# Eight groups of edges, counted back from the end from the fifth group on instead of the sixth

## The chip, the cores and the metric

The program runs on one core of a Trainium2 chip. The time is device microseconds of that core for one execution, from the runs listed below. Engines are called as in the profile: PE (matmul; its weight loads are PEld), DVE (vector), ACT (scalar), POOL (GpSimd) and SP, whose queue here only issues DMAs.

## The reference

206,250 edges, each with a row of 128 float32 and a node number `src` from 0 to 6249 in no useful order; 6,250 nodes with a row `x` of 128 float32. Everything is float32.

```
edge_aggr = zeros((n, 128)).at[src].add(edge_features)        # scatter-add of edge rows to nodes
combined  = concat([x, edge_aggr, global]) @ W_c + b_c
h = softplus(combined @ W1 + b1)
h = softplus(h @ W2 + b2)
out = layernorm(x + h @ W3 + b3)
```

## The kernel before

The scatter-add is done as a sort and a sum, the three layers follow.

**Buckets.** The nodes are cut into 32 buckets of 196. A DRAM table `rows_by` has a room of fixed size for each bucket, and sorted edge rows (128 values and the node's place in its bucket, padded to 136 floats, 544 bytes) are written into it. A *chunk* is 128 rows of one bucket, 68 KB.

**Columns, pairs, groups.** The edges lie as 1,692 columns of up to 128 edges; two columns are a pair. The 846 pairs form 8 groups, `GROUPS = (28, 72, 124, 124, 124, 128, 124, 122)`. So the groups begin at columns 0, 56, 200, 448, 696, 944, 1200 and 1448.

**Positions.** For each group, DVE and PE find where each edge goes. `node_codes(g)` splits node numbers into bucket and place. `positions(g)` records steps: compare 16 columns with the buckets (`count_set`, L498), count them with small matmuls (L509), make starts (L527 to L551), running totals for all sets (L586 to L611), then ranks inside a set (L557, L559, L576) and the target of each pair of rows (L727, L742). For a group below `GAP` these are one list of steps, and rows are placed from the front of each room. For a group from `GAP` on (`split`) there are two lists: part 0 counts, and part 1, which can begin when all groups to the end have been counted, ranks and places; the totals run over the split groups alone, and the rows are placed so that they end at the end of each room. Part 1 compares the 16 columns again. `ahead_of[g]` says which lists are worked off while group g is scattered, spread over the first 0.85 of its time by `over`.

**Sort.** Per pair, PE multiplies rows of edges by a one-hot matrix (L1155), ACT copies the result to one of six sets (L1167), and POOL scatters it to `rows_by` with an indirect DMA (L1184), 846 in all. The rows come by SP, 16 columns in a load of 1032 KB (`rows<-in_edge`).

**Fills.** Since a bucket's number of rows is random, between what is placed from the front and what is placed to the end there is a stretch of which it isn't known beforehand whether rows come. `fill_rows` writes -1 there ahead of the scatters (`rows_by<-fill`, 23 DMAs on SP). Each has a due pair, which is never later than the first pair of group `GAP`, and they are spread in time from 30 us up to 60 us ahead of the last due pair.

**Sums.** `sum_steps` plans loads of up to 8 chunks (`chunks<-rows_by` on SP, six buffers), a one-hot of the place in the bucket for up to 4 chunks (DVE, L990), a matmul for each chunk (PE, L1013) and an addition to `sums_t` (DVE, L1036). Which chunks may be loaded after how many columns is bounded from below by chance: up to `gap_at` (the first column of group `GAP`) counted from the front, after it from the end:

```
rows = (per * col - below(group_of(col))[k] if col <= gap_at
        else room * P - per * (NC - col) - left(group_of(col))[k])
```

A load waits on the SP queue for the scatters up to its column. The 196 chunks whose column is 1692 wait for all of them.

**Order.** Every step has a planned time (a scatter 1.3 us after the one before, a chunk 0.58 us of PE); the steps are sorted by it, and this order is the program of PE, DVE, ACT and SP. Sum steps that are planned after the last scatter are left for `node_layers`, which mixes them with the layers (L1358 and L1359 first layer, L1362 second, L1397 third).

Of the kernel before, what the change touches and what calls it, by code (L numbers as in the profile page):

```python
# [7 lines left out]
F32 = mybir.dt.float32  # L8
# [10 lines left out]
P = 128  # L19
# [11 lines left out]
ROWS_SD, MIXED_SD = 2.016, 0.5  # L31
LEAST, LEAST_MIXED = 3.9, 3.6
ABOVE, ABOVE_MIXED, ABOVE_LEFT = 500.0, 100.0, 1200.0
GAP = 5
TARGETS = (1, 3, 5, 8, 10, 13, 15, 18, 20, 23, 25, 28, 30, 33, 36, 38)

LOAD_COLS = 16
# [109 lines left out]
def kernel(  # L147
# [43 lines left out]
    G = len(groups)  # L191
    B_MAX = max(GROUPS)
# [12 lines left out]
    def left(g):  # L205
        n = NC - 2 * groups[g][0]
        return LEAST * ROWS_SD * n ** 0.5, LEAST_MIXED * MIXED_SD * n ** 0.5
# [3 lines left out]

    gap_at = 2 * groups[GAP][0]

# [20 lines left out]
    def untouched(k, per):  # L234
        return max(0, int(per * (NC - gap_at) - left(GAP)[k] - 2))

# [82 lines left out]
    with ExitStack() as phase:  # L319
# [3 lines left out]
        per = phase.enter_context(tc.tile_pool(name="per", bufs=2))  # L323
# [22 lines left out]
        enough = keep.tile([KB, Q_MAX], F32, name="enough")  # L346
        beyond = keep.tile([KB, G - GAP + 1, 4], F32, name="beyond")
        shift = keep.tile([KB, 2], F32, name="shift")
        whole_of = keep.tile([KB, 2, 2], F32, name="whole_of")

        def scratch(name):
            return per.tile([P, 4 * P], F32, name=name, bufs=1)

        def whole_nodes(part, n):
            node = scratch("first")[:part.shape[0], :n]
            wrap = scratch("second")[:part.shape[0], :n]
            nc.vector.tensor_copy(node, part)
            nc.vector.tensor_scalar(wrap, node, 0.0, float(N), op0=ALU.is_lt, op1=ALU.mult)
            nc.vector.tensor_add(node, node, wrap)
            nc.vector.tensor_scalar(node, node, -1.0, float(N), op0=ALU.max, op1=ALU.min)  # L360
            nc.vector.tensor_scalar(wrap, node, 0.0, float(N + 1), op0=ALU.is_lt, op1=ALU.mult)
            nc.vector.tensor_add(part, node, wrap)
            return part, node, wrap
# [7 lines left out]
        def node_codes(g):  # L371

            s0, s1 = groups[g]
            if s1 > s0:
                a, b = 2 * s0, 2 * s1
                part, node, wrap = whole_nodes(pair_i[:, a:b], b - a)
                quot_i = wrap.bitcast(I32)
                nc.vector.tensor_scalar(quot_i, part, 1.0 / BL, 0.5 / BL - 0.5, op0=ALU.mult,
                                        op1=ALU.add)
                over = scratch("third")[:PN, :b - a]  # L380
                nc.vector.scalar_tensor_tensor(node, quot_i, -float(BL), part,
                                               op0=ALU.mult, op1=ALU.add)
                nc.vector.tensor_scalar(over, node, BL - 0.5, None, op0=ALU.is_gt)
                nc.vector.scalar_tensor_tensor(over, node, -0.5, over,
                                               op0=ALU.is_lt, op1=ALU.subtract)
                nc.vector.scalar_tensor_tensor(pair_low[:, a:b], over, float(BL), node,
                                               op0=ALU.mult, op1=ALU.add)
                if b > NF:
                    c = max(a, NF)
                    nc.vector.tensor_scalar(quot_i[:, c - a:], quot_i[:, c - a:], dump[:PN], None,  # L390
                                            op0=ALU.max)
                m = a + (b - a) // BLOCK * BLOCK
                nc.vector.tensor_tensor(by_quad(pair_block[:, a:m]), by_pair(quot_i[:, :m - a]),
                                        by_pair(over[:, :m - a]), op=ALU.subtract)
                if m < b:
                    nc.vector.tensor_sub(pair_block[:, m:b], quot_i[:, m - a:], over[:, m - a:])
# [54 lines left out]
        def positions(g):  # L451
# [5 lines left out]

            split = g >= GAP

# [14 lines left out]
            def opened():  # L474
                if sets:
# [4 lines left out]
                    own["alone"] = per.tile([KB, Q_MAX], BF16, name="alone", bufs=1)  # L480
                    late, deep = ("_late", G - GAP) if split else ("", 1)
                    own["starts"] = per.tile([KB, 2, Q_MAX], F32, name="starts" + late, bufs=max(2, deep))
# [106 lines left out]
            def all_sets2():  # L589
# [4 lines left out]
                for k in range(2):  # L594
                    nc.vector.tensor_tensor_scan(total[:, k, :quads], enough[:, :quads],
                                                 small[:, 2 * k], totalled[k], op0=ALU.min, op1=ALU.add)
                    totalled[k] = total[:, k, quads - 1:quads]
                    if g in (GAP - 1, G - 1):
                        nc.vector.tensor_copy(whole_of[:, split, k:k + 1], totalled[k])
# [466 lines left out]
        def node_rows():  # L1066

            banks_of, v = {}, nc.vector

            def product_of(name, *pairs):  # L1070
                small = banks_of[name] = small_bank()
                for k, (of, by, w) in enumerate(pairs):
                    nc.tensor.matmul(small[:, k, :w], of, by, start=True, stop=True)

            def got(name, k=0, w=1):
                return banks_of[name][:, k, :w]

            b2_all = []

            def b2_rows():  # L1080
                b2_all.append(per.tile([P, P], F32, name="b2_all", bufs=1))
                v.tensor_scalar(b2_all[0], ones, b2_c, None, op0=ALU.mult)

            return [
                lambda: product_of("c", (of_weights["wc2"], cols[:, 3:4], 1)),
                lambda: product_of("fold", *((of_weights[f"wc{k}"], w_sb["w1"], D) for k in range(2))),
                lambda: v.tensor_add(c_bias, got("c"), cols[:, 0:1]),
                lambda: v.tensor_copy(fold, banks_of["fold"][:, :2, :]),
                lambda: product_of("z", (w_sb["w1"], c_bias, 1)),
                lambda: None,  # L1090
                lambda: v.tensor_add(z_bias, got("z"), cols[:, 1:2]),
                lambda: v.tensor_scalar(neg_z, z_bias, -1.0, None, op0=ALU.mult),
                lambda: product_of("b2", (w_sb["w2"], z_bias, 1)),
                lambda: None,
                lambda: v.tensor_add(b2_c, got("b2"), cols[:, 2:3]),
                lambda: v.tensor_scalar(neg_b2, b2_c, -1.0, None, op0=ALU.mult),
                b2_rows,
                lambda: product_of("b3", (b2_all[0], w_sb["w3"], D)),
                lambda: None,
                lambda: v.tensor_add(b3_all, got("b3", w=D), of_weights["b3"]),  # L1100
            ]
# [94 lines left out]
        with tc.manual_schedule(engines={ET.PE, ET.DVE, ET.Activation, ET.SP}):  # L1196
            by_part = src.rearrange("(p t) -> p t", p=P)

            def src_cols(a, b):
# [7 lines left out]
                name=nc.get_next_instruction_name(), act_func_set_id=TABLES))  # L1207
# [91 lines left out]
            when(begins[last_pair], count_over)  # L1299
            when(ends[-1], lambda: fills_left())  # L1300
            nodes, held = node_rows(), 0
            ahead_of = {g: [(g + 1, 0)] for g in range(G - 1)}
            ahead_of[GAP - 1] = [(GAP, 1)]
            for k in range(GAP, G):
                ahead_of[k - 3].insert(-1 if k == G - 1 else 1, (k, 0))
            for k in range(GAP + 1, G):
                ahead_of[k - 1] = [(k, 1)]
            ahead_of[G - 1], position_steps = [], {}
            for g in range(G):
                mine = [q for q in range(len(pieces)) if pieces[q][0] == g]  # L1310
                t0 = begins[mine[0]]
# [307 lines left out]
```

## Time and profile before

| | us |
|---|---|
| runs (3) | 1279.74, 1282.51, 1284.93; median 1282.51 |
| the profiled execution | 1280.91 |
| its span, first to last instruction | 1279.1 |
| PE busy | 1156.0 (90%) |
| DVE busy | 1047.0 (82%) |
| ACT busy | 913.4 (71%) |
| POOL busy | 883.6 (69%) |
| DMA | 381.95 MB, mean 299 GB/s |

A row of the timeline has the start, the time, engine, line and operation, what is written and read, and in brackets the idle time of the engine before it and what ended it. A row of a table by stage has the stretch, its length, busy time and count of each engine asked for, the granted share of the PE clock, the mean busy share of the 16 DMA engines, and GB/s. PE's records of a float32 matmul come in twos: 3,516 records of L1013 are 1,758 chunks.

### The profile page before, as it was taken

The numbers are of one execution on the slowest core, as the hardware profiler recorded it, in microseconds if no ns is written. First come the engines' busy times: TensorE is split into PE (matmuls) and PEld (weight loads), VectorE is DVE, ScalarE is ACT, GpSimd is POOL, SyncE is SP. The second block draws the span as 40 slices with busy tenths as digits, with TensorE's granted clock in tenths as the row PEclk, the third lists the DMA queues.
The fourth block names the chain that finished last, engine by engine and source line by source line (L and its number), as shares of the span: only waits on it lengthen the run. The fifth ranks groups of instructions, "written<-read, shape, count | busy, mean of one in ns | idle before, by whom it ended". The sixth has DMA issues, their size and how long they took to land.

```text
span 1279.1 us, 26170 instructions
## 1 busy us (share of the span) xinstructions
PE 1156.0 (90%) x8617; PEld 1098.4 (86%) x8617; DVE 1047.0 (82%) x2289; ACT 913.4 (71%) x2150; POOL 883.6 (69%) x915
## 2 busy tenths in 40 slices
PE   5777898797998899989899999999999999899893
PEld 4677788787998898989899999999999999898772
DVE  7878979986789898899888887789877767687784
ACT  5887877886776688866987878877888888303343
POOL 2777777776777777777777777777777777750334
PEclk9988999998899899999999999999999999999996
DMA  6789999999999989997999999999999999875421
GB/s 242 249 304 357 334 314 306 346 340 334 338 347 331 333 315 336 322 315 266 320 317 312 313 340 329 337 319 332 322 350 335 363 343 355 286 234 144 142 69 54
DMA packets 174635, 381.95 MB, mean 299 GB/s; under 512 B 27546, under 2 KB 118626, under 8 KB 160670
## 3 DMA queue, kind: packets, MB, share of 16 engines
q1 hardware_dynamic: 130751, 260.70, 61.7%
q0 software_dynamic: 41328, 115.65, 23.3%
q10 hardware_dynamic: 2415, 3.85, 0.8%
q8 instruction: 72, 1.18, 0.4%
q14 instruction: 69, 0.57, 0.1%
HBM read 242.47 MB, written 142.20 MB: 301 GB/s over the span
## 4 chain that ended last, share of the span: by engine, by line
PE 62%; DVE 11%; DMA 11%; ACT 6%; issue 5%; POOL 4%; SPq 0%; ACTq 0%; DVEq 0%; POOLq 0%
PE part L1013 37%; PE sorted L1155 20%; DMA rows_by<-pairs,pair 7%; POOL rows_by L1184 4%; ACT pairs L1167 3%; DMA chunks<-rows_by 3%; DVE hot L990 2%; ACT sort_hot L1142 1%; PE small L557 1%; PE small L559 1%; DVE past L727 1%; DVE sort_hot L1139 1%; PE small L1397 1%; PE sorted L1362 1%; DVE slot L576 1%
## 5 line engine op out<-in xcount | busy, mean ns | idle before, releaser
L1184 POOL DMA_INDIRECT rows_by<-pairs,pair x846 | 830.5, 982 | 289.3 <-issue 208.1
L1167 ACT COPY pairs<-sorted 64x387 f32<-64x387 f32 (+2 forms) x1144 | 543.5, 475 | 224.0 <-PE sorted L1155 165.1
L1013 PE MATMUL part<-hot,chunks 128*128 128x196 f32 x3516 | 671.0, 334 | 16.0 <-DVE sums_t L1036 9.0
L1013 PEld LDWEIGHTS part<-hot,chunks 128*128 128x128 f32 x3516 | 577.4, 191 | 25.2 <-DVE sums_t L1036 10.7
L1155 PE MATMUL sorted<-rows,sort_hot 122*128 122x129 f32 x3384 | 489.6, 284 | 36.3 <-ACT pairs L1167 25.3
L1155 PEld LDWEIGHTS sorted<-rows,sort_hot 122*128 122x128 f32 x3384 | 448.9, 196 | 45.7 <-ACT pairs L1167 35.7
L990 DVE TENSOR_TENSOR hot<-chunks,both_ps 128x784 f32<-128x784 f32 (+3 forms) x541 | 427.1, 810 | 11.7 <-DMA chunks<-rows_by 7.7
L1036 DVE TENSOR_TENSOR sums_t<-sums_t,part 128x392 f32<-128x392 f32 (+1 forms) x262 | 143.6, 548 | 115.9 <-PE part L1013 113.0
L1142 ACT ACTIVATE sort_hot<-plain,slot 122x128 f32<-122x128 f32 x684 | 227.9, 392 | 8.8 <-DVE slot L576 5.9
L1139 DVE TENSOR_TENSOR sort_hot<-slot,both_ps 122x768 f32<-122x768 f32 (+2 forms) x172 | 159.6, 928 | 7.7 <-PE sorted L1155 7.4
L1144 ACT ACTIVATE sort_hot<-sort_hot 122x768 f32<-122x768 f32 x114 | 95.9, 841 | 0.2
L1439 POOL TENSOR_SCALAR y<-y,mv,rs 128x128 f32<-128x128 f32 x40 | 31.3, 788 | 91.1 <-DVE rs L1427 90.8
L576 DVE TENSOR_REDUCE slot<-small 122x16 f32<-122x512 f32 (+2 forms) x109 | 72.9, 669 | 16.5 <-PE small L559 16.0
L498 DVE TENSOR_TENSOR pair_ib<-pair_block,plain 122x512 bf16<-122x512 bf16 (+2 forms) x157 | 63.5, 411 | 0.2
L1369 ACT ACTIVATE away<-sorted,z_bias 128x512 f32<-128x512 f32 (+2 forms) x13 | 8.5, 656 | 71.8 <-DMA chunks<-rows_by 46.4
L557 PE MATMUL small<-pair_ib,half 122*122 122x512 bf16 (+2 forms) x109 | 42.6, 391 | 9.9 <-DVE slot L576 9.6
L742 PEld LDWEIGHTS <-past 128*128 128x128 f16 x424 | 24.7, 98 | 22.6 <-DVE past L727 17.8
L742 PE MATMUL small<-jump,past 128*128 128x56 f16 (+3 forms) x424 | 28.8, 188 | 16.3 <-DVE past L727 12.1
L727 DVE TENSOR_TENSOR past<-both_ps,starts 128x512 f16<-128x512 f32 (+1 forms) x61 | 39.7, 666 | 0.2
L559 PEld LDWEIGHTS <-starts_h 128*122 128x122 bf16 x236 | 24.9, 146 | 13.2 <-issue 8.7
L727 DVE TENSOR_TENSOR past<-both_ps,starts_late 128x512 f16<-128x512 f32 (+2 forms) x49 | 32.4, 662 | 0.0
L1116 ACT COPY rows<-pair_i 122x16 f32<-122x16 f32 x106 | 22.3, 211 | 7.8 <-DMA rows<-in_edge 6.9
(161 smaller groups left out, 516.7 us busy)
## 6 DMA issues: line engine op xcount, KB each, us to landing
rows<-in_edge SPq DMA_DIRECT2D x105, 1032.0 KB
chunks<-rows_by SPq DMA_DIRECT2D x362, 136.0 KB
chunks<-rows_by SPq DMA_DIRECT2D x203, 204.0 KB
chunks<-rows_by SPq DMA_DIRECT2D x75, 272.0 KB
rows_by<-pairs,pair POOLq DMA_INDIRECT x846
rows_by<-fill SPq DMA_DIRECT2D x10, 1249.5 KB
rows_by<-fill SPq DMA_DIRECT2D x10, 714.0 KB
chunks<-rows_by SPq DMA_DIRECT2D x13, 408.0 KB
```

The costliest lines, as they stand in the source:

```text
L498: nc.vector.tensor_tensor(ib, cols.unsqueeze(2).to_broadcast([PN, m, SB, QUAD]), bucket_at[:PN].unsqueeze(1).to_broadcast([PN, m, SB, QUAD ...
L576: nc.vector.tensor_reduce(to, of, axis=mybir.AxisListType.X, op=ALU.max)
L727: nc.vector.tensor_tensor(past[:, :, a:b], twice_ps[:KB].unsqueeze(1).unsqueeze(1).to_broadcast([KB, 2, b - a, P // 2]), own["starts"][:, ...
L990: nc.vector.tensor_tensor(hot[:, q - a:q - a + m], chunks[j][:, lo:hi + 1:step, D:W].to_broadcast([P, m, BL]), iota_ps.unsqueeze(1).to_bro ...
L1013: nc.tensor.matmul(part[:, b - base_of[v], :], t[:, place_in(j, q), :D], hot[:, q - a], start=first, stop=last)
L1036: nc.vector.tensor_add(here, here, of)
L1139: return [lambda: nc.vector.tensor_tensor(hot[:PN, :2 * m], slot[:PN, at:at + 2 * m].unsqueeze(2).to_broadcast([PN, 2 * m, P]), slot_ps[:P ...
L1142: return [lambda j=j: nc.scalar.activation(hot[:PN, j], by_slot[:PN], AF.Abs, bias=slot[:PN, at + j:at + j + 1], scale=-1.0) for j in rang ...
L1144: for j in range(2 * m)] + [lambda: nc.scalar.activation(hot[:PN, :2 * m], hot[:PN, :2 * m], AF.Relu, bias=1.0, scale=-1.0)]
L1155: nc.tensor.matmul(out[:, j, :], hot[:PN, at], rows_at[col // LOAD_COLS][:PN, col % LOAD_COLS, :], start=True, stop=True)
L1167: nc.scalar.copy(sets_at[i][64 * n:64 * n + 64, lo:lo + m, h, :W], out[64 * h:64 * h + 64, :m, :])
L1184: s = nc.gpsimd.indirect_dma_start(out=dst, out_offset=bass.IndirectOffsetOnAxis(ap=at, axis=0), in_=rows[:, j].rearrange("p a b -> p (a b ...
```

## The change

`GAP` becomes 4: group 4 (columns 696 to 943) is split as groups 5 to 7 are, placed from the end and counted in advance. Which group's time counts which is now a table:

| steps | before, in the time of group | now |
|---|---|---|
| group 3, all | 2 | 2 |
| group 4, all | 3 | - |
| group 4, part 0 | - | 2 |
| group 4, part 1 | - | 3 |
| group 5, part 0 | 2 | 2 |
| group 6, part 0 | 3 | 3 |
| group 7, part 0 | 4 | 3 |
| groups 5, 6, 7, part 1 | 4, 5, 6 | 4, 5, 6 |

The scratch tiles of `node_codes` have 256 columns instead of 512 (a group has at most 256). Tiles of the split groups exist four times instead of three.

```
-GAP = 5
+GAP, COUNTED_IN = 4, {4: 2, 5: 2, 6: 3, 7: 3}
...
-            return per.tile([P, 4 * P], F32, name=name, bufs=1)
+            return per.tile([P, 2 * B_MAX], F32, name=name, bufs=1)
...
-            ahead_of = {g: [(g + 1, 0)] for g in range(G - 1)}
-            ahead_of[GAP - 1] = [(GAP, 1)]
+            ahead_of, position_steps = {g: [(g + 1, 0)] if g + 1 < GAP else [] for g in range(G)}, {}
+            for k, g in COUNTED_IN.items():
+                ahead_of[g].append((k, 0))
             for k in range(GAP, G):
-                ahead_of[k - 3].insert(-1 if k == G - 1 else 1, (k, 0))
-            for k in range(GAP + 1, G):
-                ahead_of[k - 1] = [(k, 1)]
-            ahead_of[G - 1], position_steps = [], {}
+                ahead_of[k - 1].append((k, 1))
```

`gap_at` follows from `GAP`: column 696 instead of 944. The fills' due pairs and the columns after which chunks may be loaded follow from that.

## The prediction

> **What bounds the kernel now.** I read the page's slices first, then the groups, then busy time by stage, then the end of the timeline. Slices first (tenths of 40 slices of 32 us):
> ```profile
> PE   5777898797998899989899999999999999899893
> POOL 2777777776777777777777777777777777750334
> L1184 POOL DMA_INDIRECT rows_by<-pairs,pair x846 | 830.5, 982 | 289.3 <-issue 208.1
> ```
> POOL is flat at 7 until 1120 us: one scatter after another, 0.98 us each and then mostly a pause that waits for nothing ("issue"). Two neighbours give the pitch, and the last of the 846 shows the end of this stage:
> ```profile
> 1119.21 0.98 POOL L1184 DMA_INDIRECT rows_by<-pairs,pair  x1 [0.30 <-issue]
> 1120.49 0.97 POOL L1184 DMA_INDIRECT rows_by<-pairs,pair  x1 [0.30 <-issue]
> ```
> So a scatter takes 1.28 us at best, and 846 of them 1083 us. Where is more spent? The scatters alone, by stage (columns: stretch and its us, POOL busy and count, clock, DMA share, GB/s):
> ```profile
> 152.00:282.00 130.00, 98.67 (x101) 0.96 0.93 326
> 282.00:473.00 191.00, 138.16 (x141) 0.95 0.95 334
> 473.00:640.00 167.00, 127.17 (x130) 1.00 0.90 314
> 640.00:960.00 320.00, 244.15 (x250) 1.00 0.95 327
> ```
> Count times 1.28 against the stretch: 282 to 473 us holds 141 scatters, 180.5 us of 191, so 10.5 us are lost there; 130 and 250 scatters fill 167 and 320 us, so after 473 nothing is lost. The loss stands where the fills, 20 MB in twenty large ones, are written:
> ```profile
> rows_by<-fill SPq DMA_DIRECT2D x10, 1249.5 KB
> rows_by<-fill SPq DMA_DIRECT2D x10, 714.0 KB
> 283.08 0.46 SPq L293 DMA_DIRECT2D rows_by<-fill  x1
> 286.33 5.74 SPq L293 DMA_DIRECT2D rows_by<-fill  x1
> 296.65 0.97 POOL L1184 DMA_INDIRECT rows_by<-pairs,pair  x1 [3.17 <-DMA rows_by<-pairs,pair]
> 298.93 0.97 POOL L1184 DMA_INDIRECT rows_by<-pairs,pair  x1 [1.31 <-DMA rows_by<-pairs,pair]
> 438.35 0.97 POOL L1184 DMA_INDIRECT rows_by<-pairs,pair  x1 [1.92 <-ACT pairs L1167]
> ```
> Two fills 3 us apart, and 10 us later POOL waits for the landing of its own scatters. Later it waits for ACT's copies, that is for rows that PE sorted late.
>
> From 640 to 960 us PE is full as well (all engines: PE, weight loads, DVE, ACT, POOL), so there POOL sets the pace with PE level beside it; in the two rows below those, the sums of L1013 alone (PE, weight loads):
> ```profile
> 473.00:640.00 167.00, 155.51 (x1235) 150.72 (x1234) 146.42 (x320) 133.26 (x322) 127.17 (x130) 1.00 0.90 314
> 640.00:960.00 320.00, 318.64 (x2398) 313.90 (x2397) 267.16 (x473) 253.91 (x606) 244.15 (x250) 1.00 0.95 327
> 473.00:640.00 167.00, 90.86 (x474) 76.27 (x472) 1.00 0.90 314
> 640.00:960.00 320.00, 212.81 (x1115) 179.95 (x1114) 1.00 0.95 327
> ```
> A chunk is two of these records. Last the tail on PE, from the last matmul of the sort on, and the first load there that needs every scatter:
> ```profile
> 1102.09 6.47 PE L1013 MATMUL part<-hot,chunks 128*128 128x196 f32 x38
> ...
> 1115.49 1.59 PE L1013 MATMUL part<-hot,chunks 128*128 128x196 f32 x8 [1.26 <-DVE sums_t L1036]
> 1120.21 27.39 PE L1013 MATMUL part<-hot,chunks 128*128 128x196 f32 x162 [3.12 <-DVE sums_t L1036]
> 1147.44 1.02 PE L1358 MATMUL sorted<-x_t,fold 128*128 128x512 f32 x2
> 1130.13 0.32 SPq L293 DMA_DIRECT2D chunks<-rows_by  x1
> 1137.70:1249.00 111.30, 69.65 (x394) 65.27 (x392) 1.00 0.42 124
> ```
> 27.39 us for 162 records is 0.338 us a chunk. The last 196 chunks (392 records) need all 846 scatters; they begin at 1137.8, 16.3 us after the last scatter ended, and from there to the end at 1279.1 are 141 us that this change leaves as they are.
>
> **The change, step by step.**
>
> Chunks. With the split at column 696, not 944, a bucket is sure of 60 + 2.84 rows a column by the formula in the kernel, not of 2.84 a column - 242: 300 rows or 2.4 chunks more between those columns, so sums are recorded earlier. After the last sort matmul PE has:
> ```order
> L1155 MATMUL sorted<-rows,sort_hot 128x129 x2
> L1013 MATMUL part<-hot,chunks 128x196 x19
> L1293 MATMUL small<-most_of,ones 1x48
> L1013 MATMUL part<-hot,chunks 128x196 x101
> L1358 MATMUL sorted<-x_t,fold 128x512
> ```
> before, and now:
> ```order
> L1155 MATMUL sorted<-rows,sort_hot 128x129 x2
> L1013 MATMUL part<-hot,chunks 128x196 x21
> L1293 MATMUL small<-most_of,ones 1x48
> L1013 MATMUL part<-hot,chunks 128x196 x52
> L1356 MATMUL sorted<-x_t,fold 128x512
> ```
> 120 chunks ahead of the first layer became 73: 47 chunks, 15.9 us of PE at 0.338, went ahead of the last sort matmul, into 473 to 640 us. As 196 chunks end the list in both, 91 before them became 44.
>
> What that is worth is not 15.9 us. The 196 wait for the last scatter at 1121.5. Now they begin at 1137.8. With 44 chunks (14.9 us) and the two waits (4.4 us) PE is through at 1121, and the next thing late is the load. The shortest way from scatter to sum is seen at the very first load: scatter 44, the load, its product.
> ```profile
> 78.78 0.98 POOL L1184 DMA_INDIRECT rows_by<-pairs,pair  x1 [0.30 <-issue]
> L293 SPq DMA_DIRECT2D chunks<-rows_by x693: 319/423/2455, 85.9 to 1228.5; - x174
> L1013 PE MATMUL part<-hot,chunks x3516: 327/329/696, 96.0 to 1248.5; 128*128 128x196 f32 x196
> ```
> 6.1 us from its end to the load, 10.1 to the product: 16.2, a gain of nothing. At the end the load took 8.6 us to issue, as PE still worked off older chunks in all six buffers, and 7.7 to the product. The shorter of each: 6.1 + 7.7 = 13.8 us, a gain of 2.5. I allow the issue to fall to 5, since the queue stands empty there, and take 3.6; ends 0 and 6. So 47 chunks taken from the tail bring 3.6 us, unless the scatters end earlier.
>
> PE in the middle. 473 to 640 us had 236 chunks and 11.5 us idle; 47 more, 15.9 us, fill it. It is then like 640 to 960, with 557 chunks on 250 scatters (2.23 each; now (236 + 47) / 130 = 2.18), where POOL lost nothing. On SP their loads stand ahead of loads of rows as they do after 640. So I cost it at nothing; the cover is PE's level pace, and without it up to 15.9 us.
>
> Counting on DVE. Group 4 is now counted apart from its ranks, so its sets are compared twice:
> ```profile
> L498 DVE TENSOR_TENSOR pair_ib<-pair_block,plain x157: 219/418/460, 6.8 to 925.7; 122x512 bf16<-122x512 bf16 x149, 122x256 bf16<-122x256 bf16 x6, 122x128 bf16<-122x128 bf16 x2
> L548 DVE CAST odd<-odd_i 128x32 bf16<-128x32 int32 (+3 forms) x28 | 5.6, 200 | 1.0
> 152.00:282.00 130.00, 110.79 (x941) 103.94 (x940) 113.32 (x281) 101.08 (x242) 98.67 (x101) 0.96 0.93 326
> ```
> 16 more at 0.418 is 6.7 us. The counting moves too: group 4's from group 3's time to group 2's, group 7's from group 4's to group 3's; one such count is some 16 us (16 compares are 6.7, and about 50 small ones like L548, 0.2 each). Group 2's time, 152 to 282 us, has 16.7 us of DVE free, and gets 16: DVE is then full. Group 4's time loses 16 and gains the 47 chunks' compares. I cost this at 0 to 5 us and take 1, as PE still has 19 us idle in that stretch.
>
> Fills. The same 23 fills have to be done before group 4, not group 5. On SP around one load of chunks, before (fill is a constant of -1; 112x3x952 are the 1249.5 KB):
> ```order
> L293 DMA rows<-in_edge 128x2064
> L293 DMA rows_by<-fill 112x3x952
> L293 DMA chunks<-rows_by 128x544
> L293 DMA rows<-in_edge 128x2064 x2
> L293 DMA rows_by<-fill 112x3x952
> L293 DMA chunks<-rows_by 128x2x408
> ```
> and around the same loads now:
> ```order
> L293 DMA rows<-in_edge 128x2064
> L293 DMA rows_by<-fill 112x3x952
> L293 DMA chunks<-rows_by 128x544
> L293 DMA rows<-in_edge 128x2064
> L293 DMA rows_by<-fill 112x3x952 x2
> L293 DMA rows<-in_edge 128x2064
> L293 DMA chunks<-rows_by 128x2x408
> ```
> Before, these are the first two of the ten large fills, now the last three. So each moved up past many loads, and nearly every load of rows now queues behind a fill. They are planned for 30 to 276 us, not 30 to 422, and the ten large and the last two small ones fall between 152 and 282. There and after it were, before:
> ```profile
> rows_by<-fill SPq DMA_DIRECT2D x3, 1249.5 KB
> rows_by<-fill SPq DMA_DIRECT2D x3, 714.0 KB
> ...
> rows_by<-fill SPq DMA_DIRECT2D x7, 1249.5 KB
> rows_by<-fill SPq DMA_DIRECT2D x2, 408.0 KB
> ```
> 152 to 282 us moved 326 GB/s at a share of 0.93, so full is 351. Its fills were 6.3 MB (a 238 KB one with them) and become 13.6: 326 x 130 us is 42.4 MB, and 49.7 MB at 351 GB/s take 141.5 us, 11.5 lost. 2.5 of these I let the lead of the sorted rows cover: 9, on top of the 1 lost now. From 282 to 473 all 9.8 MB go, 51 GB/s, and with them the 10.5 us as far as fills made them; I keep 1 for late rows (the 438.35 row). Ends: 3 to 19 us lost early, 5 to 10.5 regained late. I take 9 - 9.5 = -0.5.
>
> The Trainium skill speaks against that loss: DMA: Bandwidth & Descriptors, Specifications, puts the fabric's ceiling at 435 GB/s. By it 49.7 MB fit into the stretch (382 GB/s), and the term would be -9.5 instead of -0.5; that is the first rival. The same table names about 358 GB/s for a core's share of HBM, and the trace's 351 is nearer to that.
>
> Scratch of 256 columns, not 512: a tile's size alone, with the same instructions on it; nothing.
>
> Sum, against the profiled run's own 1280.9 us (span 1279.1 and 1.8 around it): -3.6 + 0 + 1 - 0.5 is -3.1, so 1278, 4.5 under the median of 1282.5, which stands 1.6 above the profiled run.
>
> **Rivals.**
> - The fills fit: the early stretch absorbs them. For it: a DMA share of only 0.93 there; against it, the 3.17 us wait after two close fills. Then the scatters end 10.5 us earlier, less the 1: 1280.9 - 3.6 - 9.5 = 1268.
> - The fills crowd: each of ten costs 2 us, as two close ones cost 3.9 (3.17 and 1.31, less the 0.30 of each pause). That is 19 over the 1 lost now; 1280.9 + 19 - 9.5 - 3.6 + 1: 1288.
> - PE has no room, slower: the 47 chunks stand ahead of sort matmuls, PE's queue is in order, and from 640 on it is full, so nothing is made up. For it: 318.64 of 320. If none of the 11.5 us idle can be used, scatters end 15.9 us later, less some 3 us by which sorting leads: 1280.9 + 13 - 3.6 = 1290. It decides once more than 3.6 us are not absorbed.
>
> **Numbers.** Half a per cent, 6.4 us, is about what a measurement can tell: 1276.1 and 1288.9. My forecast 0.50 (own range 1273 to 1282, 0.15 of it under 1276.1); fills fit 0.23 (1262 to 1273); crowd 0.15, 0.05 of it above 1288.9; no room 0.12, 0.10 of it above. Faster 0.38, same 0.47, slower 0.15. The range leaves about 0.1 at each end: 1265 to 1289.
>
> **What would show it.** Right: scatters at 1.28 us from about 290 us on; loss moved to 150 to 280; PE full from 473 on; a gap on PE of 10 us or more before the 196 chunks, which begin about 13 us after the last scatter. Wrong: scatters losing time between 473 and 640 (PE had no room), or none lost before 280 (fills fit), or no gap.

## The result and the profile after

The changed kernel took 1295.35 us (median of 6 runs, 1292.34 to 1302.45), the kernel before 1278.88 (6 runs). The ratio is 1.0125 [1.0091, 1.0159]: slower, beyond every case that was forecast. The profiled execution of the changed kernel is 1293.01 us, its span 1291.1, 12.0 more than before.

The slices and the scatters' group on the page of the changed kernel:
```profile
span 1291.1 us, 26187 instructions
...
PE   5776897768989789999999999999999999979893
...
POOL 2777767767777666777777777777777777770334
...
L1184 POOL DMA_INDIRECT rows_by<-pairs,pair x846 | 828.8, 980 | 311.5 <-issue 206.1
```
A scatter costs what it did, but POOL's row now has 6 in it, in two places: two slices between 160 and 290 us, and three from 420 us on. POOL idles 22 us longer in all. The last scatter, from the timeline:
```profile
1140.97 0.97 POOL L1184 DMA_INDIRECT rows_by<-pairs,pair  x1 [0.31 <-issue]
```
It ends at 1141.9, where it was 1121.5: 20.5 us later. The same four stages as before show where (stretch, its us, busy time and count of PE, weight loads, DVE, ACT and POOL, then clock, DMA share, GB/s; in these stretches POOL has only scatters):
```profile
152.00:282.00 130.00, 99.08 (x853) 92.89 (x851) 115.26 (x312) 90.08 (x215) 90.87 (x93) 0.92 0.99 337
282.00:473.00 191.00, 169.42 (x1370) 164.15 (x1371) 171.85 (x447) 136.64 (x328) 132.82 (x135) 0.95 0.85 295
473.00:640.00 167.00, 163.56 (x1246) 159.99 (x1244) 138.57 (x257) 130.18 (x311) 123.84 (x127) 0.99 0.87 303
640.00:960.00 320.00, 319.49 (x2407) 315.23 (x2406) 271.88 (x460) 252.84 (x605) 243.73 (x251) 1.00 0.97 330
```
With 1.28 us for each scatter, the losses are 11.0, 18.2, 4.4 and -1.3 us (a scatter that lies over a border makes up to a microsecond of error); before they were 0.7, 10.5, 0.6 and 0. Those of the first stretch were to be looked for there. Those of the second were to go, and have grown.

DMA is full in the first (0.99) and has room in the second (0.85), so a full DMA can't be the cause of both. DVE stands at 0.89 and 0.90. Nor is the first loss the transfers' alone: in 152 to 282 us POOL waited for its own landings 5.9 us (3.2 before), and as long for ACT's copies of sorted rows (1.8 before; us, times, longest):
```profile
POOL rows_by L1184 <- ACT pairs L1167: 6.1, 8, 2.3
POOL rows_by L1184 <- DMA rows_by<-pairs,pair: 5.9, 10, 1.2
```
In the second stretch the wait that grew is the one for ACT's copies (in 426 to 500 us; before, then changed):
```profile
POOL rows_by L1184 <- ACT pairs L1167: 3.8, 6, 1.9
```
```profile
POOL rows_by L1184 <- ACT pairs L1167: 18.7, 9, 4.8
```
ACT copies what PE has sorted, and between the sort matmuls PE's program has small ones that wait for DVE in turn. Three rows of the changed kernel's timeline show one such wait, the sort matmuls that come after it on PE, and POOL's wait:
```profile
445.49 0.38 PE L557 MATMUL small<-pair_ib,half 122*122 122x512 bf16 x1 [2.70 <-DVE slot L576]
...
448.47 1.34 PE L1155 MATMUL sorted<-rows,sort_hot 122*128 122x129 f32 x6
...
451.10 0.97 POOL L1184 DMA_INDIRECT rows_by<-pairs,pair  x1 [4.80 <-ACT pairs L1167]
```
And DVE alone in the worst 56 us:
```profile
430.00:486.00 56.00, 53.07 (x131) 0.91 0.63 215
```
L557 and L576 are the ranks of group 4, part 1. From 430 to 486 us DVE is busy 53.1 of 56 us, and the DMA queues, with a share of 0.63, wait. In 426 to 500 us all 16 steps of these ranks are made, and PE's L557 waits 7.9 us for DVE (the group's busy us and mean ns, then idle time before it); the kernel before makes no ranks in that stretch, its own were done by 426:
```profile
L557 PE MATMUL small<-pair_ib,half 122*122 122x512 bf16 (+1 forms) x16 | 6.3, 395 | 8.1 <-DVE slot L576 7.9
```
The compares say why they come late (L498 in the second stretch, DVE's us and count, before and then changed):
```profile
282.00:473.00 191.00, 12.91 (x32) 0.95 0.95 334
```
```profile
282.00:473.00 191.00, 24.51 (x60) 0.95 0.85 295
```
Of the 28 more, 16 are the second compare of one group; most of the rest are compares of group 2's time that were not done by 282 us. The granted clock is 0.95 in both rows, so a lower clock over the stage isn't the cause.

The end did better than forecast. PE behind the last sort matmul, and the load that needs every scatter:
```profile
1123.96 7.13 PE L1013 MATMUL part<-hot,chunks 128*128 128x196 f32 x42
...
1131.19 7.90 PE L1013 MATMUL part<-hot,chunks 128*128 128x196 f32 x46
...
1143.66 5.41 SPq L293 DMA_DIRECT2D chunks<-rows_by  x7
...
1147.53 12.38 PE L1013 MATMUL part<-hot,chunks 128*128 128x196 f32 x58 [8.44 <-DVE hot L990]
```
The load goes out 1.7 us after the last scatter (8.6 before), its product begins 3.9 us behind it: 5.6 us instead of 16.3. From there to the end it takes 143.6 us (141.3 before). So the span grew by 20.5 - 10.7 + 2.3 = 12.1, which is what was measured.

### The profile page after: what moved, and what is told of

Read it like the earlier page. It is cut to its first block, busy times and chain, and to the rows that moved or that the text cites. A ratio compares the mean times of both kernels' runs of the same rounds, so it can differ in the third digit from the quotient of the medians.

```text
span 1291.1 us, 26187 instructions
## 1 busy us (share of the span) xinstructions
PE 1154.3 (89%) x8617; PEld 1101.2 (85%) x8617; DVE 1054.2 (82%) x2301; ACT 912.5 (71%) x2150; POOL 881.6 (68%) x915
## 4 chain that ended last, share of the span: by engine, by line
PE 68%; DVE 17%; DMA 8%; issue 3%; ACT 2%; POOL 1%; SPq 0%; DVEq 0%; ACTq 0%
PE part L1013 39%; PE sorted L1155 22%; DMA chunks<-rows_by 7%; DVE hot L990 3%; DVE sort_hot L1139 1%; DVE slot L576 1%; DVE past L727 1%; POOL rows_by L1184 1%; PE small L557 1%; PE small L559 1%; DVE pair_ib L498 1%; DVE sums_t L1036 1%; ACT pairs L1167 1%; PE small L1395 1%; DMA rows_by<-pairs,pair 1%
## 5 line engine op out<-in xcount | busy, mean ns | idle before, releaser
L576 DVE TENSOR_REDUCE slot<-small 122x16 f32<-122x512 f32 (+2 forms) x109 | 72.6, 666 | 12.7 <-PE small L559 12.5
L498 DVE TENSOR_TENSOR pair_ib<-pair_block,plain 122x512 bf16<-122x512 bf16 (+2 forms) x173 | 70.1, 411 | 0.2
L557 PE MATMUL small<-pair_ib,half 122*122 122x512 bf16 (+2 forms) x109 | 43.1, 395 | 18.1 <-DVE slot L576 18.0
L727 DVE TENSOR_TENSOR past<-both_ps,starts_late 128x512 f16<-128x512 f32 (+1 forms) x65 | 42.9, 661 | 0.8 <-PE small L742 0.8
L559 PEld LDWEIGHTS <-starts_h_late 128*122 128x122 bf16 x249 | 24.3, 136 | 15.1 <-issue 9.5
L559 PEld LDWEIGHTS <-starts_h 128*122 128x122 bf16 x174 | 19.0, 150 | 15.0 <-issue 12.1
```

The costliest lines, as they stand in the source:

```text
L498: nc.vector.tensor_tensor(ib, cols.unsqueeze(2).to_broadcast([PN, m, SB, QUAD]), bucket_at[:PN].unsqueeze(1).to_broadcast([PN, m, SB, QUAD ...
L559: nc.tensor.matmul(pr[:, q * QUAD * NB:(q + 1) * QUAD * NB], own["starts_h"][:, q0 + q:q0 + q + 1].to_broadcast([KB, PN]), ident_h[:KB, :N ...
L576: nc.vector.tensor_reduce(to, of, axis=mybir.AxisListType.X, op=ALU.max)
```

## Experiments

They were to tell apart three parts of the change: the fills' pace, the counting on DVE and the sums brought forward. In three of the five series every kernel took about 1600 us (medians of 1592 to 1636; the kernel before 1593 to 1621); they are told at the end of this section. All ratios are to the kernel before in the same series.

| kernel | median us (runs) | before | ratio, interval |
|---|---|---|---|
| changed, again | 1298.10 (4) | 1280.13 (7) | 1.0129 [1.0079, 1.0179] |
| before, fills to 276 us | 1294.93 (5) | 1280.13 (7) | 1.0120 [1.0093, 1.0147] |
| before, group 7 counted earlier | 1296.05 (4) | 1280.61 (7) | 1.0112 [1.0067, 1.0156] |
| changed, sums as before | 1309.33 (4) | 1280.61 (7) | 1.0232 [1.0183, 1.0281] |
| changed, groups 4 and 6 counted earlier | 1295.22 (4) | 1280.13 (7) | 1.0110 [1.0085, 1.0134] |
| changed, fills to 326 us | 1292.18 (4) | 1280.13 (7) | 1.0078 [1.0051, 1.0104] |

**The changed kernel once more**, with the first series of the others.

> The changed kernel once more, to stand beside the other kernels of this series on one chip. Where the kernel before takes about 1279 us, 1295 (16 more); on a chip where TensorE waits more for its instructions and the kernel before takes about 1600 us, POOL has room between the scatters and the second loss (VectorE's counts) stays while the fills' is covered: 0.5 to 1.0% slower than before.

18 us above before; the result stands, on a second occasion. How far two profiles of one kernel differ is seen here too (scatters in the first two stages):
```profile
152.00:282.00 130.00, 89.04 (x91) 0.89 0.99 338
282.00:473.00 191.00, 134.02 (x136) 0.95 0.84 290
```
13.5 and 16.9 us are lost, 11.0 and 18.2 in the first profile. Differences of 2 or 3 us in one stage say nothing below.

**The fills alone.** The kernel before with the fills' pace of the changed one:
```
-            done_by = FIRST + SCATTER * todo[-1][0] - SLACK
+            done_by = FIRST + SCATTER * 240 - SLACK
```


> The kernel before, with one edit: its fills of the output with zeros spread over 30 to 276 us as in the changed kernel, not to 432. By the theory that the early loss of the changed kernel (18.1 us at scatter 220, where the kernel before had lost 7.7) is the fills' crowding, it is seen here too: 15 to 20 us lost at number 220, part of it regained behind 300 us, and the time 0 to 8 us above the kernel before. By the rival that the counts moved there made it (VectorE busy 115 of 130 us), the scatters lose 8 to 10 us at number 220 and the time is 4 us or more below the kernel before.

(The fills meant are those of `rows_by` with -1; neither the output nor zeros are concerned.)

The scatters by stage, then DVE by stage, then the last scatter:
```profile
152.00:282.00 130.00, 88.74 (x91) 0.92 0.99 341
282.00:473.00 191.00, 142.94 (x146) 0.97 0.88 306
```
```profile
152.00:282.00 130.00, 102.67 (x244) 0.92 0.99 341
282.00:473.00 191.00, 168.74 (x408) 0.97 0.88 306
```
```profile
1126.95 0.97 POOL L1184 DMA_INDIRECT rows_by<-pairs,pair  x1 [0.30 <-issue]
```
13.5 us are lost from 152 to 282 (0.7 before), 4.1 from 282 to 473 (10.5 before): 12.8 more early, 6.4 regained late, and the last scatter is 6.5 us late. DVE has less to do there than in the kernel before (102.67 us), so the early loss isn't its. What POOL waited for in 152 to 282 us, before and with the fills moved:
```profile
POOL rows_by L1184 <- DMA rows_by<-pairs,pair: 3.2, 8, 1.1
```
```profile
POOL rows_by L1184 <- DMA rows_by<-pairs,pair: 18.0, 19, 2.6
```
POOL waits for the landing of its own scatters, behind the fills. The time was more than expected (14.8 us, not 0 to 8). The profiled execution, 1288.2 us, is the fastest of the five. Its profile shows 7 us of the price, and what the other four lost beyond it no profile shows.

**One count alone.** The kernel before, with group 7 counted in group 3's time instead of group 4's. `GAP` stays 5, group 4 is counted and ranked in one go, the fills and the sums stay; the scratch tiles have 256 columns, as in the changed kernel. Written as the lists that are worked off in each group's time:
```
 ahead_of[2]: (3 whole), (5, part 0)
-ahead_of[3]: (4 whole), (6, part 0)
+ahead_of[3]: (4 whole), (6, part 0), (7, part 0)
-ahead_of[4]: (7, part 0), (5, part 1)
+ahead_of[4]: (5, part 1)
```


> The kernel before, with one edit: group 7 is counted in group 3's time, as in the changed kernel, and not in group 4's. Group 4 is still counted and ranked in one go, the fills go to 432 us and the sums as before. By the theory that the amount of counting makes the second loss (about 16 us of VectorE's work moved into 282 to 473 us, where it had some 15 to 20 us free in all), part of that loss appears: 4 to 10 us more lost by scatter 360 than before's 15.2, and a time 4 to 10 us above before. By the rival that not the amount but the order makes it (group 4's ranks can't begin before group 7 is counted), little is lost here, where group 4's ranks come first: 0 to 3 us.

The scatters by stage, the last of them, and POOL's wait for ACT's copies in 426 to 500 us:
```profile
152.00:282.00 130.00, 97.42 (x100) 0.95 0.92 321
282.00:473.00 191.00, 127.69 (x130) 0.92 0.91 317
```
```profile
1136.14 0.97 POOL L1184 DMA_INDIRECT rows_by<-pairs,pair  x1 [0.30 <-issue]
```
```profile
POOL rows_by L1184 <- ACT pairs L1167: 15.4, 9, 5.7
```
The early stage is as before (2.0 us lost). From 282 to 473 24.6 us are lost instead of 10.5, the wait for ACT's copies is there (3.8 us before), and the last scatter is 15.6 us late. A count of some 16 us, moved ahead by one group's time, costs 15.4: nothing of it found room. That was more than either theory allowed. Here group 4's ranks come first and wait for no count, so the amount is enough to make the loss. In the changed kernel, group 3's time gets one count and gives one away, and gains by itself the second compare of 6.7 us, beside what group 2's time leaves over; there the ranks come behind both counts. How much this order adds was not tried apart.

**Counts earlier still.** The changed kernel with two of its counts moved ahead by one group's time:
```
-COUNTED_IN = {4: 2, 5: 2, 6: 3, 7: 3}
+COUNTED_IN = {4: 1, 5: 2, 6: 2, 7: 3}
```


> The changed kernel with group 4 counted in group 1's time and group 6 in group 2's (5 in group 2's and 7 in group 3's as they were), so that one fewer group is counted ahead of group 4's ranks. By the theory that the second loss of the scatters (13.5 us in scatters 300 to 345) is VectorE's, which must count groups 6 and 7 and make all of group 4's ranks in one group's time, a good half of it goes: 5 to 7 us left in it, and about 1286 where the kernel before takes 1279. By the rival that transfers or sums make that loss, it stays above 10 us.

The scatters by stage, then DVE:
```profile
152.00:282.00 130.00, 83.84 (x85) 0.95 0.94 316
282.00:473.00 191.00, 140.14 (x144) 0.96 0.90 317
```
```profile
152.00:282.00 130.00, 111.59 (x290) 0.95 0.94 316
282.00:473.00 191.00, 168.93 (x425) 0.96 0.90 317
```
The second loss fell from 18.2 to 6.7 us, as the counting theory says; the first rose from 11.0 to 21.2, which it didn't foresee, and the time is the changed kernel's. The sums stand where they stood, so the second loss is not theirs. The work has only been moved to where, beside the fills, it costs as much.

One reckoning holds the five kernels together: DVE's busy time in a stage for each scatter in it. Before, the two stages had 113.32 us for 101 and, from its row for DVE alone,
```profile
282.00:473.00 191.00, 161.93 (x388) 0.95 0.95 334
```
161.93 for 141. The one-count kernel's DVE rows are
```profile
152.00:282.00 130.00, 111.69 (x278) 0.95 0.92 321
282.00:473.00 191.00, 164.25 (x422) 0.92 0.91 317
```

| kernel | DVE us a scatter, 152 to 282 | lost there | 282 to 473 | lost there |
|---|---|---|---|---|
| before | 1.12 | 0.7 | 1.15 | 10.5 |
| fills to 276 us | 1.13 | 13.5 | 1.16 | 4.1 |
| one count moved | 1.12 | 2.0 | 1.26 | 24.6 |
| changed | 1.24 | 11.0 | 1.27 | 18.2 |
| counts earlier | 1.31 | 21.2 | 1.17 | 6.7 |

The number of scatters stands in both columns, so a loss from any cause raises the quotient where DVE works on, and the table alone is no proof; the edits are. Reckoned ahead, from the row of the kernel before, the moved count makes (161.93 + 16) / 141 = 1.26 us, as was then seen.

Where DVE has up to 1.17 us of work for a scatter of 1.28, most of the losses go with the fills (0.7 and 10.5 us before, 13.5 with the fills moved into the stage); the 4.1 and 6.7 us lost from 282 on without fills are not explained by either. At 1.24 or more it needs nearly the whole pitch, and in these ten stages its share of time never rose above 0.90 (171.85 of 191), though it reached 0.95 over the 56 us shown above. With 0.90 taken as the most, an estimate from these rows, 1.26 us of work take 1.40: about 0.12 us lost a scatter, 16 us over the 130 of the one-count kernel, of the 24.6 it loses. In the changed kernel's first stage the two causes lie over each other: fills alone lose 13.5 there, fills and counts together 11.0 or 13.5. So the counts that ran there, while the fills held POOL back, cost nothing more that can be seen.

**The fills a little later.** The changed kernel with its fills spread over 30 to 326 us:
```
-FILLS, SLACK = 30.0, 60.0
+FILLS, SLACK = 30.0, 10.0
```


> The changed kernel with its fills spread over 30 to 326 us, not 276. By the theory that the fills' rate over 152 to 282 us (337 GB/s, the queue full at 340) takes about 11 us from the scatters there, a sixth more time for them gives back about half: 5 to 7 us less lost at scatter 220, the second loss (300 to 345) as in the changed kernel, and a time 4 to 7 us below the changed kernel's. By the rival that VectorE's counts make the early loss, nothing changes against the changed kernel.

1292.18, 5.9 us under the changed kernel of the same series, with intervals that overlap. The profiled execution, at 1297.1 the slowest of the four, shows no gain:
```profile
152.00:282.00 130.00, 93.16 (x95) 0.92 0.96 340
282.00:473.00 191.00, 130.77 (x133) 0.94 0.86 301
```
8.4 and 20.8 us are lost, as far from the changed kernel's 11.0 and 18.2 as its two profiles are from each other. Inconclusive.

**The sums as before.** The changed kernel, where a chunk between columns 696 and 944 is still counted on from the front only, so that its loads come no earlier than before:
```
-    if col <= gap_at
+    if col <= 2 * groups[5][0]
```


> The changed kernel, whose sums may not run ahead into the last four groups but only as far as the kernel before let them, so that 287 chunks, not 240, are left after the last matmul of the sort. By the theory that the tail's gain of 8 to 11 us comes from these chunks alone, and that the sums brought forward cost nothing in the middle, the scatters lose what they lose in the changed kernel (36 to 40 us) and the tail is that of before: about 1304, 8 to 11 us above the changed kernel. By the rival that the sums brought forward are part of the second loss, that loss shrinks by 5 us or more and the time stays within 3 us of the changed kernel's.

The scatters in the second stage, POOL's wait for ACT's copies in 426 to 500 us, and the end of the scatters on POOL and on PE:
```profile
282.00:473.00 191.00, 133.18 (x135) 0.95 0.85 293
```
```profile
POOL rows_by L1184 <- ACT pairs L1167: 18.4, 8, 4.8
```
```profile
1144.67 0.98 POOL L1184 DMA_INDIRECT rows_by<-pairs,pair  x1 [0.30 <-issue]
...
1145.20 28.81 PE L1013 MATMUL part<-hot,chunks 128*128 128x196 f32 x162 [4.71 <-DVE sums_t L1036]
```
The second loss is the same (18.2 us, and 18.4 of waits for ACT's copies in 426 to 500), so the sums brought forward cost nothing in the middle. PE has its old work behind the last scatter again: from there to the end of the span (1305.2) it takes 159.6 us, where the changed kernel takes 149.2 and the kernel before 157.6. The 47 chunks are worth 8 to 10 us at the end, and no other effect of theirs is seen here.

**Where every kernel took about 1600 us.** Twelve runs fell in such series. Four kernels above and three others ran there:

| kernel | median us | before | ratio, interval |
|---|---|---|---|
| before, fills to 276 us | 1623.81, 1595.42 | 1621.38, 1592.51 | 1.0012 [0.9976, 1.0047], 1.0001 [0.9961, 1.0040] |
| before, fills to 354 us | 1593.64 | 1593.13 | 1.0024 [0.9991, 1.0057] |
| before, fills to 472 us | 1595.47 | 1593.13 | 1.0022 [0.9995, 1.0048] |
| changed, fills to 326 us | 1622.34, 1592.47 | 1621.38, 1592.51 | 0.9997 [0.9964, 1.0030], 0.9978 [0.9946, 1.0010] |
| before, group 7 counted earlier | 1599.83 | 1593.13 | 1.0035 [1.0000, 1.0071] |
| changed, sums as before | 1633.44, 1598.48, 1600.17 | 1621.38, 1592.51, 1593.13 | 1.0084 [1.0049, 1.0118], 1.0020 [0.9990, 1.0050], 1.0036 [1.0006, 1.0066] |
| changed, all four counts earlier | 1635.92, 1603.30 | 1621.38, 1592.51 | 1.0112 [1.0047, 1.0177], 1.0076 [1.0039, 1.0114] |

The last has `COUNTED_IN = {4: 1, 5: 1, 6: 2, 7: 2}`; the fills to 354 us have 300 in the place of 240 in the edit above, those to 472 us `SLACK = 10.0` in the kernel before. These are planned times: the kernel before has 422, and its last fill went out at 432.4; the expectations count from the latter and say 482.

Fills to 276 us, in the two series:

> The kernel before, with nothing changed but the planned times of its 23 fills: spread from 30 to 276 us as in the changed kernel, not to 422. Theory B, the fills: the scatters lose some 11 us more up to 300 us and win back what they lost after it, at most 10; net 0 to +8, 1279 to 1287 us, with the DMA share at 0.98 or more from 152 to 282 us. Theory A, the counting: the fills cost nothing by themselves; the early loss of the changed kernel came of counting group 4 there; no change, 1279 us, and under 5 us lost by 300 us.

> The kernel before, with one edit: its fills of the output with zeros spread over 30 to 276 us as in the changed kernel, not to 432. Counts, sums and tail stay as before. By the theory that the early loss of the changed kernel (18.1 us at scatter 220, where the kernel before had lost 7.7) is the fills' crowding, it is seen here too: 15 to 20 us lost at number 220, of which the scatters regain what the fills took from them behind 300 us (before lost 8.4 from number 220 to the end), so that the time is 1279 to 1287. By the rival that the counts moved there made it (VectorE busy 115 of 130 us), the scatters lose 8 to 10 us at number 220 and the time is 1275 or less.

The changed kernel with fills to 326 us:

> The changed kernel, but fills are due 10 us ahead of the scatter that needs them, not 60, so they spread from 30 to 326 us and not to 276. Theory B: of the 17 us lost between scatters 100 and 220 some 5 go, 1288 us. Theory A: no change, 1293 us. If fills that come close to their scatters hold POOL up, slower.

> The changed kernel with its fills spread over 30 to 326 us, not 276 (a smaller slack before the same point). By the theory that the fills' rate over 152 to 282 us (337 GB/s, the queue full at 340) takes about 11 us from the scatters there, a sixth more time for them gives back about half: 5 to 7 us less lost at scatter 220, some of it lost again in scatters 220 to 300, the second loss (300 to 345) as in the changed kernel, and the time 1288 to 1292. By the rival that VectorE's counts make the early loss, nothing changes: 1295.

The one count, and the sums as before:

> The kernel before, with one edit: group 7 is counted in group 3's time, as in the changed kernel, and not in group 4's. Group 4 is still counted and ranked in one go, the fills go to 432 us and the sums as before. By the theory that VectorE is the second bound there (about 16 us of counting moved into 282 to 473 us, where it had some 15 to 20 us free in all), part of the scatters' second loss of the changed kernel appears: 4 to 10 us more lost by scatter 360 than before's 15.2, and a time 4 to 10 us above before. By the rival that not the amount but the order makes that loss (group 4's ranks can't begin before group 7 is counted), little is lost here, where group 4's ranks come first: 0 to 3 us.

> The changed kernel, but up to column 944 the chunks are counted as sure by the bound from the front as before, which claims fewer: the sums stand where they stood, 91 chunks again and not 44 between the last sort matmul and the 196 that need every scatter. If the earlier sums are worth the 10.7 us by which the 196 now start sooner after the last scatter (5.6 us, 16.3 before): 8 to 11 us slower, 1303 us. If PE's extra work in the middle had cost the scatters their time: the scatters end earlier and the time is 1293 us or less.

> The changed kernel, whose sums may not run ahead into the last four groups but only as far as the kernel before let them (the front bound to column 944 in place of 1256), so that TensorE has about 90 chunks more to multiply after the last sort. By the theory that the changed kernel's early gap between last scatter and first late product closed from 16.3 to 5.6 us because fewer chunks are left there, this gives back the tail: about 10 us, 1305. By the rival that TensorE's sums in the middle are what delays the scatters of 300 to 345, the second loss of 13.5 us shrinks and the time falls below 1293.

> The changed kernel, whose sums may not run ahead into the last four groups but only as far as the kernel before let them, so that 287 chunks, not 240, are left after the last matmul of the sort. By the theory that the tail's gain of 8 to 11 us comes from these chunks alone, and that the sums brought forward cost nothing in the middle, the scatters lose what they lose in the changed kernel (36 to 40 us) and the tail is that of before: about 1304, 8 to 11 us above the changed kernel. By the rival that the sums brought forward are part of the second loss, that loss shrinks by 5 us or more and the time stays within 3 us of the changed kernel's.

(In the second of the texts on the sums, the bound is column 944 in place of 696, and the chunks are 47 more, some 90 in all.)

All four counts earlier:

> The changed kernel, but groups 4 and 5 are counted in the time of group 1 and groups 6 and 7 in that of group 2, so that only the ranking of group 4 is left for the time of group 3. Theory A, the counting: of the 20 us by which the scatters end later, some 13 stand between scatters 300 and 345, where VectorE is full for 58 us because the counts of groups 6 and 7 come first and the ranking of group 4 is pushed into the rest of group 3's time. Then these 13 us go: about 1280 us, and between scatters 300 and 345 under 4 us are lost. Theory B, the fills: the late loss is left over from the crowded fills; then nothing goes, 1293 us, and the late loss stays near 16 us. Counting more in groups 1 and 2 may cost up to 5 us there.

> The changed kernel with the four groups counted one group's time earlier (4 and 5 in group 1's, 6 and 7 in group 2's); fills and sums as in the changed kernel. By the theory that the second loss of the scatters (13.5 us in scatters 300 to 345, 426 to 500 us) is VectorE's, which has all of group 4's ranks, pairs and slots to make after group 7 has been counted in the same group's time, that loss goes: the scatters lose under 4 us behind number 300 and the kernel ends near 1280 where the kernel before ends at 1279. By the rival that the loss at 426 to 500 comes from the queue of the transfers or from the sums on TensorE, it stays above 10 us and the time near 1295. A way between: the counts, moved into the time of the fills, lose on the scatters of 60 to 200 what they give back later, which shows as more loss before number 220 than the changed kernel's 18.1.

Fills to 354 and to 472 us:

> The kernel before, with one edit: its fills end at 354 us, between its own 432 and the changed kernel's 276. By the theory that the loss grows with the rate of the fills (20 MB in 402, 324 or 246 us: 49, 61 or 81 GB/s beside the rest), about a third of what 276 us costs, since 12 of the 32 GB/s are added: some 5 us above before, and 3 to 5 us more lost by scatter 220. By the rival that there is a step, where the queue is full (351 GB/s), it costs less than 2 us.

> The kernel before, with its fills spread to 482 us instead of 432 (42 GB/s instead of 49), the other way from the change. By the theory that the loss grows with their rate, 2 to 4 us below before: 1276 to 1278. By the rival of a step, which before is already below, no difference: within 1 us. The late fills fall where VectorE is busiest (412 to 482 us), which should not matter to it.

These runs don't tell the parts at the pace of 1.28 us: only the four counts earlier (twice) and the sums as before (in two of three series) stand clear of the kernel before, by 0.4 to 1.1%. Whether the fills' price grows with their rate, or a pace slower than before's would gain, stays open. The groups of the kernel with fills to 276 us, in the first of these series, show why:
```profile
L1184 POOL DMA_INDIRECT rows_by<-pairs,pair x846 | 827.6, 978 | 623.9 <-ACT pairs L1167 319.2
...
L1013 PEld LDWEIGHTS part<-hot,chunks 128*128 128x128 f32 x3516 | 618.2, 203 | 99.7 <-issue 70.6
```
A scatter takes 0.98 us as ever, but POOL idles 624 us, not 300, and half of it waits for sorted rows: PE is busy 1297.2 us at a granted clock of 0.895, against 1160.2 at 0.968 where the same kernel took 1288.2. The scatters aren't the pace there, and fills that cost 1.2% in the other series cost nothing to be seen.

## Why the prediction was wrong

**The term on DVE failed: +1 was forecast, and the counts cost 12 to 16 us.** The step was "Group 2's time ... has 16.7 us of DVE free, and gets 16: DVE is then full. Group 4's time loses 16", and then "0 to 5 us and take 1, as PE still has 19 us idle in that stretch". Two things are wrong in it. Group 3's time, most of 282 to 473 us, got no price. It gives group 4's count away and gets group 7's, so the swap seemed free; but the second compare stays there, 15 compares of group 2's time ran over into the stretch, and group 4's ranks came behind it all. DVE was busy 161.93 of 191 us there before, and group 7's count alone, put into it, cost 15.4 us. And that PE is idle says nothing of the wait: in the rows shown its sort matmuls come after small ones that wait for DVE. A stage that reads as 85% busy had no room for 16 us; with the waits between DVE and PE it was as good as full.

In the changed kernel itself the price is the step from the fills alone: there the last scatter was 6.5 us late, here it is 20.5. The 14.0 between them are the counts', as the sums cost nothing. By the medians of that series it is less: 1298.10 against 1294.93, and the tail's gain of 8.4 on top, 11.6.

**The fills' term: the early half was right in kind, the late half was not.** "9, on top of the 1 lost now" became 12.8 with the fills alone, inside the 3 to 19 given, and by the mechanism given: waits for landings, at a DMA share of 0.99. In the changed kernel the early loss was no larger, though it waited as long for sorted rows as for landings. Of "9.5" to regain, 6.4 came: 4.1 us stay lost between 282 and 473 without fills. So -0.5 was +6.4 in the profile, and 14.8 by the medians. The rival that the fills crowd, 2 us each and +9.5 in this sum, lies between the two and came nearer than the forecast. The rival that the fills fit fell: with them moved, the stage moved 341 GB/s at a share of 0.99, so what was full there was nearer 341 than the 351 of the prediction. The 435 GB/s that the Trainium skill gives as the fabric's ceiling (DMA: Bandwidth & Descriptors, Specifications) was reached in no stage shown here; its figure of about 358 for a core's share of HBM is the nearer one, as the prediction had said. Neither 351 nor 358 is a bound for every mix of transfers: one slice of 32 us late in the scatters, on the page of the changed kernel, moved 383 GB/s.

**PE in the middle: nothing, as forecast.** PE is busy 163.56 of 167 us from 473 on, 640 to 960 us lose no scatter, and holding the 47 chunks back returned nothing: the 4.4 us lost from 473 to 640 (0.6 before) are lost with the sums as before too, where 127 scatters fell in that stage as well. The rival that was to decide on the slower side, that PE has no room, is refuted; the slower result came from elsewhere.

**The tail: right in kind, too small.** "I allow the issue to fall to 5", and 7.7 from the load to the product: they were 1.7 and 3.9. The gain there was 10.7 rather than 3.6 us, above its upper end of 6, less 2.3 given back later: 8.4. The gap on PE ahead of the 196 chunks came, with 8.44 us where 10 or more were forecast.

With sizes measured apart put in, and the one count's price for DVE's term, the forecast's own sum is -8.4 + 0 + 15.6 + 6.4 = +13.6: 1280.9 becomes 1294.5, and the profiled execution took 1293.0 (the median 1295.35). That it comes so close is in part luck: by the medians the count and the fills cost 15.4 and 14.8, and the sum would be +21.8, more than the 16.5 between the medians of the result. DVE's term was too small by 11 to 15 us by every reading. The fills' term was too small by 7 in the profiles and by 15 by the medians; which of the two it is stays open.

## What to carry to other kernels

Before work is moved on an engine that isn't the bound, add what is moved to its busy time in each stage, divide by the number of steps of the engine that sets the pace, and compare with the pace: 1.15 us of 1.28 went unseen here and 1.26 did not, and a stage busy 85% of its time had no room for 16 us more. Look at every stage that the move touches, not at the sum over them. A loss at one place may have two causes, and a transfer moved out of it gives back only its own part.

## What the runs showed that was not expected

With fewer older chunks left, the first load behind the last scatter took 1.7 us to go out and 3.9 to its product, 5.6 together, against 16.3 where older chunks held the six buffers. And the same kernel took 1280 us in some series and 1593 to 1621 in others. The kernel with fills to 276 us has profiles from both: the slow one has a lower granted clock (0.895 against 0.968) and more idle time on PE that the profile puts down to "issue"; what made that isn't settled.
